# Folding the carried state into the decay's first column, in five scans of each pass

## The chip, the cores and the metric

The kernel runs on one core of a Trainium2 chip. The metric is the time of one execution on the device, in microseconds; the median of several runs is compared. The core has engines that work side by side and wait for each other by semaphores: TensorE (PE) multiplies matrices into PSUM, VectorE (DVE), ScalarE (ACT) and GpSimd (POOL) work on elements, SyncE (SP) issues the transfers. Each engine takes its instructions in order.

## The reference, cut to what matters

The network has two layers, each a state-space mixer and an MLP, on a picture of 64 x 64 tokens with 96 channels. The change concerns the mixer of layer 1. For each of 192 inner channels and 16 states it runs a recurrence over all 4096 tokens, in four directions: by rows, by columns, and both backward.

```python
def step(h, inp):
    u_t, dt_t, B_t, C_t = inp
    dA = jnp.exp(dt_t[..., None] * A)
    h = dA * h + (dt_t * u_t)[..., None] * B_t[:, None, :]
    y = jnp.sum(h * C_t[:, None, :], axis=-1)
    return (h, y)
_, ys = jax.lax.scan(step, h0, (uT, dT, BT, CT))
```

So a state is the decay times the state before, plus an input. The four directions' states are summed for each token, multiplied by C, summed over the 16 states, and gated.

## The kernel before, in words

**Tiles.** 192 channels times 16 states are 3072 recurrences. They are worked off in 24 passes of 128 (6 groups of 32 channels, 4 passes of 4 states in each). A pass holds 128 partitions by 4096 tokens, and cuts the tokens into four parts of 1024 (`SC`), so that each of the four directions is four scans, 16 in a pass. One scan is one VectorE instruction at line 1998: `tensor_tensor_scan` with multiply and add, on a decay tile in PSUM and an input tile in SBUF. Its fourth operand is where the running state starts: 0.0 for the first part of a direction, and for the others a column of a tile, the last state of the part before (128 partitions by 1 element).

**Chains and slots.** `o` tells rows (0) from columns (1), and `e` counts 0 to 7 along both ways: 0 to 3 forward (or backward, in turn), 4 to 7 the other way. `seq` alternates between the chains: column scan m, then row scan m - 2. Scan p of `seq` therefore continues scan p - 2. In this text a slot is the place of a scan in a pass, counted from the pass's first column scan: even slot s is the column scan e = s / 2, slots 1 and 3 are row scans 6 and 7 of the pass before, and slots 5, 7, 9, 11, 13 and 15 are row scans 0 to 5. Row or column scan 4 starts again from 0.0, as scan 0 does (slots 0, 5, 8 and 13). Scans e < 4 write into the tiles h0s and h1s, the later ones in place into their input (x0s, x1s, x2s for rows, in rotation; xws for columns).

**Decays.** `decay(p + 1)` is issued just behind `scan(p)` in the program (lines 2220 to 2222): ScalarE computes exp(dt times a rate) for the next scan into one of two PSUM tiles (`two`, da in the profile), which alternate. Its tile is the one that scan p - 1 reads, so it has to wait for that scan's end. Scan e = 4 reuses the decay tile of scan e = 3, over the same tokens the other way.

**What else is in the pass.** The other work is put behind numbered scans by a written plan (`put`, `spots`, `base`), in slots: four copies on ScalarE that permute the row input for the column scans (line 1968; slots 11, 13, 15, and 4 of the next pass); GpSimd's product of B and the input (1962), its sum of the two column directions (2003) and its product with C (2026); TensorE's sums of the directions through an identity matrix (2009 and 2013, from slot 14 into the next pass's slots 0 to 6); ScalarE's fetch of these sums from PSUM in eight halves (2022; slots 0, 1, 2, 3, 5, 6, 7, 9); TensorE's sum over states (2037). In two passes of each group of channels ScalarE and TensorE also compute the gate (2069; tanh at 2078 to 2080, in slot 12), and the end of a group adds a Copy with a scale (2090), a fetch (2096) and two products. In passes late in the kernel the first parts of the output product run beside (2121 to 2127). Loads are issued by SP in the order of the same plan.

**The end phase.** The last ten scans, from `first_late` on, and the output, the MLP and the stores are ordered by a planner (`Order`), which starts from costs and leads written into the program.

Of the kernel before, what the change touches and what calls it, by code (L numbers as in the profile page):

```python
# [33 lines left out]
AF = mybir.ActivationFunctionType  # L34
# [22 lines left out]
NS = 4  # L57
SC = L // NS
# [65 lines left out]
PAIRS = HW // 2  # L124

RELU0_ACT = [(c, 0) for c in range(8)]
IN_DVE, OTHERS = (), (15, 9, 9)


# [134 lines left out]
class Net:  # L264
# [832 lines left out]
    def keep(self, instruction):  # L1097
        self.tc.keep_in_program_order(instruction)
# [378 lines left out]
    def mlp0(self, c):  # L1477
# [18 lines left out]
        def rounded(m):  # L1496
            return lambda: keep(nc.scalar.copy(at["h16", c, m], at["h", c, m]))

        def relu(m):
            h, b = ("h16", c, m), b1[:, m : m + 1]  # L1500
            if (c, m) in RELU0_ACT:
                return lambda: keep(nc.scalar.activation(at[h], at[h], AF.Relu, bias=b))
            return lambda: keep(nc.vector.tensor_scalar(at[h], at[h], b, 0.0, ALU.add, ALU.max))

        def small(m):
            return lambda: keep(nc.gpsimd.tensor_copy(at["h8", c][:, m], at["h16", c, m], saturate=False))

        for m in range(nm):
            o.add("PE", 0.45, up(m), r=[xt], new={("h", c, m): "bank", **({} if m else {("h8", c): "h8"})})
            o.add("ACT", 0.58, rounded(m), r=[("h", c, m)], new={("h16", c, m): "h16"})  # L1510
            o.add(*(("DVE", 0.58), ("ACT", 0.73))[(c, m) in RELU0_ACT], relu(m), w=[("h16", c, m)])
            o.add("POOL", 0.72, small(m), r=[("h16", c, m), ("h8", c)], w=[("h8", c, m)])
# [371 lines left out]
    def scans(self, xs, out):  # L1884
# [13 lines left out]
        nc, tc, keep = self.nc, self.tc, self.keep  # L1898
        with ExitStack() as ctx:
# [7 lines left out]
            n, ns = len(passes), 4 * NS  # L1907
# [3 lines left out]
            hs, h0, h1, xw = self.hs, self.h0, self.h1, self.xw  # L1911
# [12 lines left out]
            seq = [(0, o, e) for o, e in first]  # L1924
# [3 lines left out]
            pos = {s: p for p, s in enumerate(seq)}  # L1928
            base = [pos[i + 1, 1, 0] - ns for i in range(last)] + [pos[last, 1, 0]]
            first_late = pos[last, 1, NS]  # L1930

            def slot(i, o, e):

                way = e // NS
                return way, (i + way) % 2 == 1, turn[i % 2][way][e % NS]

            das, accs, sums = {}, {}, {}
            two = [pa.tile([P, SC], F32, tag=f"da{j}", name=f"da{j}") for j in range(2)]
# [31 lines left out]
            def decay(p):  # L1970
                i, o, e = seq[p]
                if e == NS:

                    das[p] = das[pos[i, o, e - 1]]
                    return
                das[p] = 1 - das[p - 1] if p else 0
                decay_into(p)

            def decay_into(p):
                i, o, e = seq[p]  # L1980
                g, k = passes[i]
                t, j = two[das[p]], slot(i, o, e)[2]
                keep(nc.scalar.activation(t, dts[o][:, part[j]], AF.Exp, scale=self.a6[:, g, k : k + 1]))  # L1983

            def rows(i, j):
                return xs[2] if i == 0 and j < 2 else h0

            def scan(p):
                i, o, e = seq[p]
                way, back, j = slot(i, o, e)  # L1990
                x = (xs[i % 3], xw)[o]
                h = x if way else h1 if o else rows(i, j)
                to, da, x = h[:, part[j]], two[das[p]], x[:, part[j]]
                if back:
                    to, da, x = to[:, ::-1], da[:, ::-1], x[:, ::-1]
                at = (j + 1) * SC if back else j * SC - 1
                start = 0.0 if e % NS == 0 else (h if way or o else rows(i, j - 1 + 2 * back))[:, at : at + 1]
                keep(nc.vector.tensor_tensor_scan(to, da, x, start, ALU.mult, ALU.add))  # L1998

            def add_columns(i, a):  # L2000
# [167 lines left out]
            for i in range(n):  # L2168
# [22 lines left out]
                at = base[i - 1] if i else 0  # L2191
# [28 lines left out]
            for p in range(first_late):  # L2220
                scan(p)
                decay(p + 1)
                for f, args in plan.pop(p, []):
                    f(*args)
            assert not plan
            for p in range(first_late + 1, len(seq)):
                i, o, e = seq[p]
# [4 lines left out]
            at = od.at  # L2232
# [64 lines left out]
            for p in range(first_late, len(seq)):  # L2297
                i, c, e = seq[p]
                if p > first_late and e != NS:
                    od.add("ACT", 1.12, lambda p=p: decay_into(p), w=[("da", das[p])], table="exp")  # L2300
                od.add("DVE", 2.33, lambda p=p: scan(p), r=[("da", das[p]), ("S", c, e - 1)], w=[("S", c, e)])
# [4 lines left out]
            for p in (len(seq) - 2, len(seq) - 1):  # L2306
                i, c, e = seq[p]
# [22 lines left out]
            for a in range(NS):  # L2330
                j = turn[last % 2][1][a]
# [14 lines left out]
                else:  # L2346
                    t = hs[:, part[j]]
# [3 lines left out]
                    for h in range(nh):  # L2351
                        e, cost = ((dve, 1.2), (pool, 1.5))[a in TIMES_POOL]
# [224 lines left out]
```

## Time and profile before

| What | Value |
|---|---|
| median of 3 runs | 1230.8 us (1229.6 to 1230.89) |
| the profiled execution's own time | 1231.9 us |
| its span, first to last instruction | 1229.9 us |
| TensorE clock granted, mean | 0.877 of full speed |
| VectorE busy | 1134.9 us, 92% |
| TensorE busy | 1013.7 us, 82% |
| ScalarE busy | 881.8 us, 72% |
| GpSimd busy | 842.4 us, 68% |
| scans of layer 1 at line 1998 | 382, from 306.7 us to 1174.4 us |

The profile is one execution. A group of it is a line of the program with its engine, its operation, its operands by name (out, then in) and its shape, with the count and the durations. The timeline lists instructions by their start; what stands in brackets is how long the engine had been idle before and what ended that. The chain that ended last is followed back from the last instruction to what released each step. Scans in place (x0s<-da,x0s) don't show by name whether they begin with a constant or a column; those into h0s and h1s do, because the column is of the same tile.

### The profile page before, as it was taken

The page shows a single profiled execution, that of the slowest core. Times are in us where ns is not written, and L with a number is a line of the kernel's source. Part 1 is how long each engine was busy: PE and PEld are TensorE (multiplying, and loading weights), DVE is VectorE, ACT ScalarE, POOL GpSimd, SP SyncE. Part 2 cuts the span into 40 slices and gives each one's busy share as a digit, 9 for nine tenths or more (in the row PEclk, how much of TensorE's full clock was granted, in tenths as well). Part 3 has the DMA queues.
Part 4 walks back from the last instruction along what each step waited for, and adds up shares of the span by engine and source line. Part 5 has one row for each costly group of instructions (what it writes and reads, how often), then busy time and mean ns, then how long its engine had stood idle before and what let it go on. Part 6 is the DMA issues. An engine that isn't in the chain of part 4 may idle for free.

```text
span 1229.9 us, 11118 instructions
## 1 busy us (share of the span) xinstructions
PE 1013.7 (82%) x3498; PEld 414.7 (34%) x3498; DVE 1134.9 (92%) x908; ACT 881.8 (72%) x1065; POOL 842.4 (68%) x510
## 2 busy tenths in 40 slices
PE   9997889985278877887787877889778889888986
PEld 5533334321023322222332222233224444343344
DVE  7895787788898999999999999999999999999968
ACT  5682555656568878877888777878878878887626
POOL 3002364352678888888798878987798888886756
PEclk9998989995589887889978788988789999988987
DMA  2252010476763573575734585545736766432201
GB/s 76 67 174 53 1 27 20 124 245 193 235 193 126 182 237 125 172 230 172 239 112 127 194 258 166 180 146 185 233 115 194 246 195 235 142 101 83 103 1 52
DMA packets 79132, 183.14 MB, mean 149 GB/s; under 512 B 21534, under 2 KB 34936, under 8 KB 77688
## 3 DMA queue, kind: packets, MB, share of 16 engines
q1 hardware_dynamic: 78376, 182.16, 47.6%
q8 instruction: 29, 0.48, 0.2%
q14 instruction: 39, 0.32, 0.1%
q10 hardware_dynamic: 688, 0.19, 0.1%
HBM read 159.73 MB, written 21.52 MB: 147 GB/s over the span
## 4 chain that ended last, share of the span: by engine, by line
DVE 46%; issue 11%; PE 10%; ACT 5%; DMA 2%; POOL 1%; SPq 0%; another core or an unknown queue 0%; DVEq 0%; POOLq 0%; ACTq 0%
DVE h1s L1998 14%; DVE xws L1998 13%; DVE h0s L1998 8%; PE hs L2009 4%; DVE x2s L1998 3%; DVE x0s L1998 3%; DVE x1s L1998 3%; PE hs L2013 2%; ACT da L1983 2%; ACT xws L1968 2%; DMA x2s<-bc 1%; PE eo L2123 1%; PE da L2326 1%; POOL hss L2003 1%; DMA kept<-xn 1%
## 5 line engine op out<-in xcount | busy, mean ns | idle before, releaser
L2026 POOL TENSOR_TENSOR kept<-kept,kept 128x1024 f32<-128x1024 f32 x92 | 216.7, 2356 | 82.3 <-issue 40.2
L2003 POOL TENSOR_TENSOR hss<-h1s,xws 128x1024 f32<-128x1024 f32 x96 | 228.0, 2377 | 55.2 <-DVE xws L1998 52.4
L2009 PE MATMUL hs<-h0s,ident 128*128 128x512 f32 x360 | 222.9, 705 | 27.6 <-DVE h0s L1998 24.0
L1983 ACT ACTIVATE da<-dt1s,a 128x1024 f32<-128x1024 f32 x168 | 187.5, 1117 | 71.3 <-DVE xws L1998 55.3
L1998 DVE TENSOR_TENSOR_SCAN xws<-da,xws 128x1024 f32<-128x1024 f32 x96 | 221.6, 2308 | 10.4 <-ACT da L1983 10.3
L1983 ACT ACTIVATE da<-dt0s,a 128x1024 f32<-128x1024 f32 x166 | 185.1, 1115 | 45.1 <-DVE h0s L1998 16.2
L2013 PE MATMUL hs<-hss,ident 128*128 128x512 f32 x368 | 188.1, 603 | 15.4 <-POOL hss L2003 15.3
L1998 DVE TENSOR_TENSOR_SCAN h1s<-da,h1s,xws 128x1024 f32<-128x1024 f32 x72 | 167.3, 2323 | 0.3
L2037 PE MATMUL acc<-kept,fold 128*32 128x512 f32 x368 | 87.6, 687 | 73.8 <-POOL kept L2026 73.8
L2022 ACT COPY kept<-hs 128x512 f32<-128x512 f32 x184 | 107.1, 582 | 47.0 <-PE hs L2013 46.3
L2009 PEld LDWEIGHTS hs<-h0s,ident 128*128 128x128 f32 x360 | 71.5, 216 | 152.4 <-issue 82.3
L2013 PEld LDWEIGHTS hs<-hss,ident 128*128 128x128 f32 x368 | 70.0, 194 | 116.2 <-issue 79.1
L2009 PE MATMUL hs<-x1s,ident 128*128 128x512 f32 x128 | 75.5, 675 | 14.1 <-DVE x1s L1998 14.1
L2009 PE MATMUL hs<-x0s,ident 128*128 128x512 f32 x128 | 73.6, 659 | 14.8 <-DVE x0s L1998 14.8
L1962 POOL TENSOR_TENSOR x1s<-x1s,dus 128x1024 f32<-128x1024 f32 x32 | 75.5, 2361 | 9.0 <-DMA x1s<-bc 9.0
L2009 PE MATMUL hs<-x2s,ident 128*128 128x512 f32 x120 | 69.1, 660 | 14.1 <-DVE x2s L1998 14.1
L1962 POOL TENSOR_TENSOR x2s<-x2s,dus 128x1024 f32<-128x1024 f32 x32 | 75.7, 2364 | 2.7 <-DMA x2s<-bc 2.7
L1998 DVE TENSOR_TENSOR_SCAN x0s<-da,x0s 128x1024 f32<-128x1024 f32 x32 | 73.9, 2310 | 1.1 <-ACT da L1983 1.1
L1998 DVE TENSOR_TENSOR_SCAN x1s<-da,x1s 128x1024 f32<-128x1024 f32 x32 | 73.9, 2308 | 1.1 <-ACT da L1983 1.1
L1998 DVE TENSOR_TENSOR_SCAN x2s<-da,x2s 128x1024 f32<-128x1024 f32 x32 | 73.9, 2311 | 0.6 <-ACT da L1983 0.4
L1968 ACT COPY xws<-x1s 128x1024 f32<-128x1024 f32 x32 | 63.2, 1974 | 5.4 <-POOL hss L2003 5.4
L1968 ACT COPY xws<-x2s 128x1024 f32<-128x1024 f32 x32 | 63.2, 1976 | 4.2 <-POOL x2s L1962 4.2
(374 smaller groups left out, 1887.3 us busy)
## 6 DMA issues: line engine op xcount, KB each, us to landing
kept<-bc SPq DMA_DIRECT2D x92, 512.0 KB
x2s<-bc SPq DMA_DIRECT2D x32, 512.0 KB
x0s<-bc SPq DMA_DIRECT2D x28, 512.0 KB
x1s<-bc SPq DMA_DIRECT2D x28, 512.0 KB
dus<-du SPq DMA_DIRECT2D x20, 512.0 KB
dt1s<-dt SPq DMA_DIRECT2D x20, 512.0 KB
dt0s<-dt SPq DMA_DIRECT2D x20, 512.0 KB
kept<-xn SPq DMA_DIRECT2D x24, 384.0 KB
```

What stands on the lines that cost most here:

```text
L1962: keep(nc.gpsimd.tensor_tensor(x, x, du[:, part[j]], ALU.mult))
L1968: keep(copy(grid(xw)[:, w, :], cols(xs[i % 3])[:, w, :]))
L1983: keep(nc.scalar.activation(t, dts[o][:, part[j]], AF.Exp, scale=self.a6[:, g, k : k + 1]))
L1998: keep(nc.vector.tensor_tensor_scan(to, da, x, start, ALU.mult, ALU.add))
L2003: keep(nc.gpsimd.tensor_tensor(cols(hs)[:, w, :], grid(h1)[:, w, :], grid(xw)[:, w, :], ALU.add))
L2009: keep(nc.tensor.matmul(t, self.ident, x[:, chunk(m)], start=k == 0, stop=False))
L2013: keep(nc.tensor.matmul(sums[i, m], self.ident, hs[:, chunk(m)], start=False, stop=True))
L2022: keep(nc.scalar.copy(to, sums.pop((i, j * (SC // CH) + h))))
L2026: keep(nc.gpsimd.tensor_tensor(t, t, times_c_by(i, a), ALU.mult))
L2037: keep(nc.tensor.matmul(to, self.fold4, src, start=k == 0, stop=k == NK - 1))
L2123: keep(nc.tensor.matmul(o[:, j], y[:, j:CH:4], w, start=False, stop=j == 3))
L2326: keep(nc.tensor.matmul(o[:, j], y[r, 2 * k + j : CH : 4], w[r], start=first and j == 0, stop=end and j == 1))
```

## The change

In five slots of a pass (2, 3, 4, 7 and 9) the scan begins with the constant 1.0 and no longer with the carried column. So that the result is the same, ScalarE first multiplies the first column of the decay tile (the last one, for a backward scan) by the carried column: the scan's first step is then 1.0 times (decay times state), plus the input. The multiplication is a Copy with a scale for each partition, on 128 x 1 elements in place in PSUM, issued right behind the decay of that scan. `CARRIED` names the slots, counted from another origin ((p - 14) modulo 16, so 0, 1, 2, 5, 7). Scans 0 and 4, which start a direction, and scan 3, whose decay tile is read again by scan 4, are kept out by a condition, as are the first pass's early scans and the end phase; 112 scans are left.

```diff
+CARRIED = (0, 1, 2, 5, 7)
...
             first_late = pos[last, 1, NS]
+            carried = [p for p in range(ns, first_late) if (p - 14) % ns in CARRIED and seq[p][2] not in (0, NS - 1, NS)]
...
+            def carry(p):
+                i, o, e = seq[p]
+                way, back, j = slot(i, o, e)
+                at = (j + 1) * SC if back else j * SC - 1
+                h = (xs[i % 3], xw)[o] if way else h1 if o else rows(i, j - 1 + 2 * back)
+                return h[:, at : at + 1]
+
+            def carry_into(p):
+                if p in carried:
+                    at = SC - 1 if slot(*seq[p])[1] else 0
+                    t = two[das[p]][:, at : at + 1]
+                    keep(nc.scalar.activation(t, t, AF.Copy, scale=carry(p)))
...
-                at = (j + 1) * SC if back else j * SC - 1
-                start = 0.0 if e % NS == 0 else (h if way or o else rows(i, j - 1 + 2 * back))[:, at : at + 1]
+                start = 0.0 if e % NS == 0 else 1.0 if p in carried else carry(p)
                 keep(nc.vector.tensor_tensor_scan(to, da, x, start, ALU.mult, ALU.add))
...
             for p in range(first_late):
                 scan(p)
                 decay(p + 1)
+                carry_into(p + 1)
                 for f, args in plan.pop(p, []):
                     f(*args)
```

## The prediction

> **What bounds the kernel now.** I read the page first, its busy times and its chain that ended last:
>
> ```profile
> PE 1013.7 (82%) x3498; PEld 414.7 (34%) x3498; DVE 1134.9 (92%) x908; ACT 881.8 (72%) x1065; POOL 842.4 (68%) x510
> DVE 46%; issue 11%; PE 10%; ACT 5%; DMA 2%; POOL 1%; SPq 0%; another core or an unknown queue 0%; DVEq 0%; POOLq 0%; ACTq 0%
> ```
>
> VectorE is both the busiest engine and the main part of the chain. Next, the view of the scan's line (count; shortest/median/longest ns; first and last start), and the same for the two scans of another line:
>
> ```profile
> L1998 DVE TENSOR_TENSOR_SCAN h1s<-da,h1s,xws x72: 2319/2322/2349, 309.1 to 1144.8; 128x1024 f32<-128x1024 f32 x72
> L1998 DVE TENSOR_TENSOR_SCAN h1s<-da,xws x24: 2259/2260/2279, 306.7 to 1131.5; 128x1024 f32<-128x1024 f32 x24
> its engine sat idle before it (us, times) until:
>   ACT da L1983: 13.0, 11
> L1832 DVE TENSOR_TENSOR_SCAN x2s<-x1s,x0s x1: 2282/2282/2282, 297.3 to 297.3; 128x1024 f32<-128x1024 f32 x1
> L1832 DVE TENSOR_TENSOR_SCAN x2s<-x1s,x2s,x0s x1: 2350/2350/2350, 299.7 to 299.7; 128x1024 f32<-128x1024 f32 x1
> ```
>
> A scan that begins with a column of a tile takes 2322 ns, one that begins with the constant 0.0 takes 2260: 62 ns less, 68 at line 1832. All 382 scans idle for only 13 us in front of them. The timeline of VectorE in one pass says whether the 62 ns are also steps of the chain (start, duration):
>
> ```profile
> 412.83 2.26 DVE L1998 TENSOR_TENSOR_SCAN h1s<-da,xws 128x1024 f32<-128x1024 f32 x1
> 415.01 2.32 DVE L1998 TENSOR_TENSOR_SCAN x2s<-da,x2s 128x1024 f32<-128x1024 f32 x1
> 417.26 2.32 DVE L1998 TENSOR_TENSOR_SCAN h1s<-da,h1s,xws 128x1024 f32<-128x1024 f32 x1
> 419.50 2.32 DVE L1998 TENSOR_TENSOR_SCAN x2s<-da,x2s 128x1024 f32<-128x1024 f32 x1
> 421.74 2.32 DVE L1998 TENSOR_TENSOR_SCAN h1s<-da,h1s,xws 128x1024 f32<-128x1024 f32 x1
> ```
>
> They are: 2.18 us from start to start after the constant form, 2.24 after the other, each starting a little before the one ahead has ended. A pass of 12 and 4 takes 35.63 us (412.83 to 448.46), so x and x - 0.061 with 16x - 0.244 = 35.63: 2.242 and 2.181 us.
>
> What ScalarE does meanwhile, for slots 4 to 6 of that pass, and its dependent pair in another pass:
>
> ```profile
> 419.61 1.12 ACT L1983 ACTIVATE da<-dt1s,a 128x1024 f32<-128x1024 f32 x1 [0.61 <-DVE h1s L1998]
> 420.76 0.59 ACT L2022 COPY kept<-hs 128x512 f32<-128x512 f32 x1
> 421.85 1.12 ACT L1983 ACTIVATE da<-dt0s,a 128x1024 f32<-128x1024 f32 x1 [0.51 <-DVE x2s L1998]
> 422.91 1.98 ACT L1968 COPY xws<-x0s 128x1024 f32<-128x1024 f32 x1
> 424.79 1.12 ACT L1983 ACTIVATE da<-dt1s,a 128x1024 f32<-128x1024 f32 x1
> ...
> 505.98 0.39 ACT L2079 ACTIVATE kept<-z 128x256 f32<-128x256 f32 x1
> 506.41 0.51 ACT L2080 ACTIVATE kept<-kept,columns 128x256 f32<-128x256 f32 x1
> ```
>
> The decay of a slot starts when the scan two slots earlier has ended (417.26 + 2.32 = 419.58) and gives back its buffer. It is ready at 420.73, and its scan starts at 421.74: 1.01 us to spare. I worked this spare time out for every slot of passes 1 to 22. In the five slots of the change it is 0.92 to 1.01 us, but for four of slot 2 (0.46, 0.60, 0.68, 0.77) and one of slot 9 (0.89). The tight slots are others: slot 6, behind the permuting copy (0.20 to 0.25), slots 1 and 15 (about 0.27).
>
> **What the Trainium skill says.** (1) "DVE: scalar operands, raw-bit mode, write accounting and state across instructions", section Scalar operands: a scalar is either a [P,1] operand read per partition or a constant inside the instruction. It gives no price; the two forms in the trace do. (2) "VectorE: DVE Perf Modes", section The DRAIN you can't avoid: an instruction that reads what the one before it on its engine wrote needs a semaphore, which costs nothing extra on VectorE. For ScalarE the trace has 0.04 us between the dependent pair above (505.98 + 0.39 to 506.41). (3) "ScalarE: Activation LUTs", section Table sets: copy is in every table set, so a Copy between two Exp loads no table. The trace agrees: line 2090's Copy runs between decays without a load.
>
> **The change, part by part.**
> *Removed:* 112 scans lose the column operand. Slots 2, 3, 4, 7 and 9 (column scans 1 and 2, the row scan 7 of the pass before, row scans 1 and 2), in 22 or 23 passes each: 22 + 22 + 23 + 23 + 22. At 0.061 us: 6.83 us of VectorE. That 1.0 is as cheap as 0.0 isn't shown; both are constants of the instruction, so I take the whole 0.061 (ends: 0 and 0.068).
> *Added:* 112 ScalarE instructions on one column, with a per-partition scale, in place in PSUM. No row has this shape. By "ScalarE: Activation LUTs", section What ACT_TABLE_LOAD costs, 186 ns + 0.833 per element + 93 for a pointer operand is 280 ns as an estimate (the same formula gives 1132 for the decay, which takes 1118). The nearest row, line 2400 with 4 columns and a pointer, takes 299. With 0.02 to 0.04 behind the decay I take c = 0.32 us; ends 0.19 (the page's overlap of 93 ns taken off) and 0.42 (PSUM read as well as written). ScalarE's busy time grows by some 33 us.
> *On the path?* Its column comes from the scan two slots earlier, for whose end the decay has waited anyway, so it adds no wait but the one on its decay. Its own scan keeps 0.92 - 0.32 = 0.60 us to spare; the worst slot 2 keeps 0.14. Queued behind it are a fetch (line 2022) and the next decay. Behind slot 4's, from 419.61 on: the fetch can start 1.05 + c later, the next decay 0.48 after that, at 1.53 + c. That decay's buffer now comes free 2.18 after 419.61, so up to c = 0.65 nothing moves. Past that it would delay slot 6, whose spare 0.20 falls to 0.14 because scan 4 is shorter: slot 6 stalls from c = 0.79. The fetch feeds POOL's product and PE's second buffer; PE is at the next half chunk then. Where PE paces that fetch, in the worst pass (698.1), the decay is late by 0.04 us and slot 6 keeps 0.12. So at both ends of c the cost is nothing; the cover is ScalarE's idle 0.5 to 0.6 us in front of each decay. Without that cover it would be 112 x 0.32 = 36 us.
> *Waits:* the scan waits for ScalarE as before, for a later instruction. Later writers of the carried column must also wait for ScalarE's read, long past. Line 1998 has 194 semaphore instructions of 21 ns in VectorE's queue, without a mark on the 2.24 steps. I take 0.
> *Where the gain is given back:* wherever a chain that does not pass through VectorE ends in one of the stalls. One of them, in the view of the chain:
>
> ```profile
> 479.73 5.31 PE hs L2009 x6
> ...
> 504.96 6.40 DMA kept<-xn
> ```
>
> and where it ends, in VectorE's timeline:
>
> ```profile
> 517.70 2.35 DVE L1998 TENSOR_TENSOR_SCAN x2s<-da,x2s 128x1024 f32<-128x1024 f32 x1 [0.15 <-ACT da L1983]
> ```
>
> From 479.73 PE sums without pause until 504.95, then the gate's input is loaded and ScalarE's tanh steps follow, and slot 15 waits. Earlier scans in that pass only wait longer here: all 5 places are lost. Likewise pass 1 (stall at 372.0, PE from 337.6): 3. The stalls at 945.6, 981.3, 1088.4 and 1126.3 begin with scan slot 8 (929.66, 965.68, 1072.66, 1111.37): slot 9 is lost in each, 4. The stall at 1152.3 in the end phase follows PE sums from 1133.7: the last 4. Together 16 of 112, 0.98 us.
> *Sum:* 96 x 0.061 = 5.86 us. The profiled execution has a span of 1229.9 and a time of 1231.9, 1.1 above the median of the runs: 1231.9 - 5.9 = 1226.0 for it, and 1230.8 - 5.9 = 1224.9 on the median. I say 1225.0 us (-0.47%). What a measurement here can tell from no change is about 0.2%, 2.5 us.
>
> **Rivals.**
> *A, absorbed:* PE is 82% busy, and in gate passes VectorE already waits for it. If the shorter passes (35.32) run into PE's sums, POOL's products or late fetches in all 12 passes with tanh steps instead of 6, 12 x 5 = 60 of the 112 places are lost: 52 x 0.061 = 3.2, or 1227.6; if other passes are hit too, 1229. Against it: in the 6 others slot 14 keeps its full 0.93 to 0.95.
> *B, no saving:* the constant 1.0 may cost what the column costs, or the shorter form only owe its time to being a chain's first. Then 1230.8. Against it: line 1832 and both directions show the same difference.
> *C, slower:* the in-place multiply waits for PSUM's acknowledgment much longer than the pair above for SBUF's. Its place is between decay and scan, in all five slots. It decides from c = 1.02, where the spare of about 0.98 and the gained 0.061 are used up (0.02 of hand-over counted). At c = 1.1 each place loses 0.08, 112 x 0.08 = 9 us: 1240. For it: no row shows a PSUM read behind a PSUM write on ScalarE. Against it: that would be more than three times any small ScalarE row.
> *D, more:* PE's clock (0.877 on average) falls elsewhere against the passes and some of the 10 us of stalls vanish: 1222.
>
> **How the numbers follow.** Forecast (4.5 to 7 us saved) 0.64; A 0.14, of it 0.08 clear of 2.5 us; B 0.06; C 0.11; D 0.05. Faster 0.64 + 0.08 + 0.05 = 0.77, same 0.06 + 0.06 = 0.12, slower 0.11. The range leaves out C, B and half of D, some 0.2: from 1222.8 to 1229.3 us. The forecast alone: 1223.7 to 1226.3.
>
> **What would show it.** Right: 45 of the 72 scans h1s<-da,h1s,xws lose their column operand and take 2260; a pass takes 35.32 us; a new ScalarE group of 112 at about 0.3 us, with nobody waiting long for it; the stall at slot 15 of the pass that began at 484 grows from 0.24 to about 0.5. Wrong: constant-one scans at 2320 (B), VectorE idle before slots 2, 3, 4, 7, 9 or 6 in most passes (C), or new stalls in slots 14 and 15 of many gate passes (A).

## The result and the profile after

The changed kernel takes 1225.6 us, the median of 12 runs (1223.4 to 1232.9), against 1230.85 for the kernel before (12 runs, 1227.6 to 1235.3). The ratio is 0.9964, with an interval of 0.9948 to 0.9979: 0.36% faster, 4.4 us, give or take 1.9. A repetition gave 1225.2 us and 0.9959 (0.9944 to 0.9974). The profiled execution took 1229.0 us, one of the longer ones; its span is 1227.0, 2.9 below that of before.

The page's busy times, and its chain that ended last:

```profile
PE 1016.3 (83%) x3498; PEld 415.0 (34%) x3498; DVE 1128.4 (92%) x908; ACT 905.9 (74%) x1177; POOL 841.3 (69%) x510
DVE 38%; PE 16%; issue 9%; ACT 7%; DMA 3%; POOL 1%; another core or an unknown queue 0%; DVEq 0%; SPq 0%; POOLq 0%; ACTq 0%
```

VectorE has lost 6.5 us of work, ScalarE has gained 24.1 us and 112 instructions. The chain leans less on VectorE (46% before) and more on TensorE (10% before). That says nothing yet of the gain: in the version further down that only adds the multiplications, and is no faster, VectorE has 37% of the chain and TensorE 14%. The scan is at line 2012 now, the decay at 1985, the fetch at 2036, the permuting copy at 1970. The view of the scan's line, cut (shortest/median/longest ns):

```profile
L2012 DVE TENSOR_TENSOR_SCAN h1s<-da,xws x69: 2262/2268/2273, 307.0 to 1137.3; 128x1024 f32<-128x1024 f32 x69
...
L2012 DVE TENSOR_TENSOR_SCAN h1s<-da,h1s,xws x27: 2324/2330/2350, 309.3 to 1141.7; 128x1024 f32<-128x1024 f32 x27
...
its engine sat idle before it (us, times) until:
  ACT da L1985: 15.8, 13
```

45 of the 72 column scans with a carried column have become constant ones, and the two forms differ by the same 62 ns. Every scan is 6 to 8 ns longer in this trace than in that of before, the untouched ones too; the steps from start to start are not. The view of the new line, 2001, cut to one of its five groups:

```profile
L2001 ACT ACTIVATE da<-da,h1s x45: 236/236/238, 346.0 to 1136.4; 128x1 f32<-128x1 f32 x45
...
who waited for it (us, times):
  PEld hs L2023: 0.5, 2
```

236 ns each, and no scan is recorded as waiting for it. Now the steps, in VectorE's timeline of pass 3 (the passes count from 0; it is the pass whose timeline the prediction shows), from slot 2 on, with a stall that wasn't there before:

```profile
417.12 2.26 DVE L2012 TENSOR_TENSOR_SCAN h1s<-da,xws 128x1024 f32<-128x1024 f32 x1
419.30 2.27 DVE L2012 TENSOR_TENSOR_SCAN x2s<-da,x2s 128x1024 f32<-128x1024 f32 x1
421.49 2.26 DVE L2012 TENSOR_TENSOR_SCAN h1s<-da,xws 128x1024 f32<-128x1024 f32 x1
423.67 2.27 DVE L2012 TENSOR_TENSOR_SCAN h0s<-da,x0s 128x1024 f32<-128x1024 f32 x1
426.59 2.35 DVE L2012 TENSOR_TENSOR_SCAN h1s<-da,h1s,xws 128x1024 f32<-128x1024 f32 x1 [0.66 <-ACT da L1985]
```

Slots 2, 3 and 4 now take 2.18 us from start to start. Then slot 6 comes 0.74 us late. ScalarE in the same pass:

```profile
415.17 1.12 ACT L1985 ACTIVATE da<-dt1s,a 128x1024 f32<-128x1024 f32 x1
416.33 0.24 ACT L2001 ACTIVATE da<-da,h1s 128x1 f32<-128x1 f32 x1
416.49 0.59 ACT L2036 COPY kept<-hs 128x512 f32<-128x512 f32 x1
...
421.93 0.59 ACT L2036 COPY kept<-hs 128x512 f32<-128x512 f32 x1 [0.70 <-PE hs L2027]
422.41 1.12 ACT L1985 ACTIVATE da<-dt0s,a 128x1024 f32<-128x1024 f32 x1
...
425.37 1.12 ACT L1985 ACTIVATE da<-dt1s,a 128x1024 f32<-128x1024 f32 x1
```

The decay of slot 2 ends at 416.29, the multiplication follows 0.04 later and is done at 416.57: c = 0.28 us. The fetch behind it starts 1.32 us after the decay's start, where 1.05 was usual. The stall of slot 6 has another reason: the fetch at 421.93 had waited 0.70 us for TensorE, and the decay behind it, the permuting copy and the decay of slot 6 (425.37) were late with it.

To compare traces I use two sums. The stretch is from the first scan's start to the last one's. The stalls are what each step exceeds 2.242 us by (2.181 after a constant), where that is over 0.06; the first four steps of the kernel are left out.

| | stretch, us | ordinary pass, us | stalls, us |
|---|---|---|---|
| before | 867.7 | 35.63 | 18.3 |
| after | 864.5 | 35.32 | 21.9 |

Between these two traces, the 112 places saved 112 x 0.061 = 6.83 us of steps; the stalls grew by 3.6; 3.2 are left. They grew by 0.74 in pass 3 (slot 6), 0.59 in pass 5, 0.64 in pass 17, 0.28 in pass 18, 0.88 in pass 22, and by less elsewhere. The stall at the end of pass 5, which stood in the prediction with 0.15 us of idle time, is now

```profile
518.02 2.35 DVE L2012 TENSOR_TENSOR_SCAN x2s<-da,x2s 128x1024 f32<-128x1024 f32 x1 [0.55 <-ACT da L1985]
```

### The profile page after: what moved, and what is told of

Read it like the earlier page. It is cut to its first block, busy times and chain, and to the rows that moved or that the text cites. A ratio compares the mean times of both kernels' runs of the same rounds, so it can differ in the third digit from the quotient of the medians.

```text
span 1227.0 us, 11219 instructions
## 1 busy us (share of the span) xinstructions
PE 1016.3 (83%) x3498; PEld 415.0 (34%) x3498; DVE 1128.4 (92%) x908; ACT 905.9 (74%) x1177; POOL 841.3 (69%) x510
## 4 chain that ended last, share of the span: by engine, by line
DVE 38%; PE 16%; issue 9%; ACT 7%; DMA 3%; POOL 1%; another core or an unknown queue 0%; DVEq 0%; SPq 0%; POOLq 0%; ACTq 0%
DVE xws L2012 11%; DVE h1s L2012 10%; PE hs L2023 7%; DVE h0s L2012 7%; PE hs L2027 4%; ACT da L1985 3%; DVE x2s L2012 3%; DVE x1s L2012 2%; DVE x0s L2012 2%; ACT xws L1970 2%; DMA kept<-xn 2%; DMA dt<-hss 1%; POOL hss L2017 1%; ACT kept L2036 1%; PE acc L2051 1%
## 5 line engine op out<-in xcount | busy, mean ns | idle before, releaser
L2012 DVE TENSOR_TENSOR_SCAN h1s<-da,xws 128x1024 f32<-128x1024 f32 x69 | 156.5, 2268 | 0.0
L1964 POOL TENSOR_TENSOR x0s<-x0s,dus 128x1024 f32<-128x1024 f32 x28 | 66.3, 2368 | 0.0
```

What stands on the lines that cost most here:

```text
L1964: keep(nc.gpsimd.tensor_tensor(x, x, du[:, part[j]], ALU.mult))
```

## The experiments

Diffs are against the changed kernel, unless said otherwise.

**The constant alone.**

```diff
-                carry_into(p + 1)
```

> The 112 scans begin with the constant 1.0, but the multiplication on ScalarE is left out, so the carried state is missing from these scans. My theory (the gain is VectorE's 0.061 us per place, ScalarE's part is nearly free, the rest is given back in stalls that TensorE paces): an ordinary pass of 35.32 us as with the change, and a time within 1.5 us of the changed kernel's, 1224 to 1226. Rival 1 (ScalarE's added work costs a good part of the gain): 3 us or more faster than the changed kernel, 1222 or less. Rival 2 (a constant saves nothing): 1231, as before.

Measured: 1225.6 us, ratio to before 0.9956 (0.9936 to 0.9975); ordinary passes 35.32 us. This is the changed kernel's time without any of its work on ScalarE. The interval, 1222.9 to 1227.7 us, leaves out rival 1's 1222 and rival B's 1230.8.

**The multiplication alone.**

```diff
-                    keep(nc.scalar.activation(t, t, AF.Copy, scale=carry(p)))
+                    keep(nc.scalar.activation(t, t, AF.Copy, scale=self.one))
...
-                start = 0.0 if e % NS == 0 else 1.0 if p in carried else carry(p)
+                start = 0.0 if e % NS == 0 else carry(p)
```

> The scans keep their column operand; ScalarE does the 112 extra instructions in the same places, but multiplies by a column of ones. My theory: 1231, within 1.5 us of before, passes of 35.63 us. Rival 1: 1233 or more. An extra instruction takes 236 ns in both.

Measured: 1231.45 us, ratio 0.9998 (0.9983 to 1.0014); passes of 35.63 us. 112 instructions of 236 ns cost nothing that can be measured; the interval reaches from 2.1 us less to 1.7 us more. Its trace has stalls of 20.2 us, with VectorE's steps unchanged: 2 us more than the trace of before, at the same time within the interval.

**Every place.**

```diff
-                carry_into(p + 1)
...
-                start = 0.0 if e % NS == 0 else 1.0 if p in carried else carry(p)
+                start = 0.0 if e % NS == 0 else 1.0 if ns <= p < first_late else carry(p)
```

> Every scan from the second pass to the end phase begins with a constant (1.0 in place of each column) and nothing is multiplied, so the carried state is missing in all of them. 268 places at 0.061 us are 16.3 us of VectorE's time, and an ordinary pass is 16 x 2.181 = 34.90 us. My theory: some 48 places lie between the start of a chain without VectorE and a stall and are lost, so 13 us are left, 1218; if the six other passes with tanh steps stall too, 9 us, 1222. Rival 2: 1231. Rival 3 (TensorE or another engine is the bound as soon as passes are shorter than 35.3): 1225, no better than the change, with idle time before many scans.

Measured: 1218.6 us, ratio 0.9907 (0.9886 to 0.9929). VectorE's timeline, first scans of two passes:

```profile
410.98 2.26 DVE L2012 TENSOR_TENSOR_SCAN h1s<-da,xws 128x1024 f32<-128x1024 f32 x1
...
445.88 2.26 DVE L2012 TENSOR_TENSOR_SCAN h1s<-da,xws 128x1024 f32<-128x1024 f32 x1
```

34.90 us, 16 x 2.181. 12.2 of 16.3 us arrive, between the 13 and the 9 expected; a part of them may come from the granted clock, 0.883 on average in these six runs and 0.877 in those of the kernel before. TensorE and the others are not the bound of an ordinary pass even there, and the 0.061 us hold for all 12 places of a pass. The stalls are 23.0 us in this trace.

**Twice the work on ScalarE, and four times.**

```diff
                     keep(nc.scalar.activation(t, t, AF.Copy, scale=carry(p)))
+                    keep(nc.scalar.activation(t, t, AF.Copy, scale=self.one))
```

and with the added line three times, in a loop.

> The change with every multiplication on ScalarE followed by a second one by a column of ones, so c (from the decay's end to the end of the last of them) is 2 x 0.28 = 0.56 us. The prediction's limits were 0.65 for the decay of slot 5, 0.79 for a stall of slot 6, 0.92 to 1.01 for the five slots themselves. My theory: still free, 1224.5 to 1227, ordinary passes of 35.32 us. Rival 1 (ScalarE's work counts): 1229 or more.

> Four dependent instructions in each place (the multiplication and three by ones), c = 1.12 us. My theory: past the spare of 0.94 to 1.01; each place waits some 0.15 to 0.2 us for ScalarE, and slot 6 another 0.3: 112 x 0.17 + 22 x 0.3 = 26 us slower than the change, 1250 (1240 to 1260), with line 2001 as releaser in front of scans in all five slots. If the spare is larger than I read from the trace: below 1235.

Measured: twice 1225.5 us, ratio 0.9946 (0.993 to 0.9961), most passes at 35.32 or up to 0.12 above; c is 0.54 us. Four times 1265.2 us, ratio 1.0261 (1.023 to 1.0291). So the cover is there: a second multiplication costs nothing that the times show. Some cost can't be ruled out: four passes with the gate (2, 6, 10 and 14) got stalls of 0.1 us in slot 15 that the traces of the change don't have, and the 12 runs had a granted clock of 0.886 on average, against 0.878 for the kernel before, which may hide a cost of 1 or 2 us. (An estimate: by the two groups of runs at the end of this section, 0.008 of clock goes with some 3 us.) Four times is far past the limit. But it is 15 us worse than I expected. Its ScalarE and its VectorE in pass 3:

```profile
418.50 1.13 ACT L1985 ACTIVATE da<-dt0s,a 128x1024 f32<-128x1024 f32 x1
...
419.93 0.77 ACT L2003 ACTIVATE da<-da,columns 128x1 f32<-128x1 f32 x3
...
421.10 1.13 ACT L1985 ACTIVATE da<-dt1s,a 128x1024 f32<-128x1024 f32 x1
```

```profile
420.74 2.29 DVE L2014 TENSOR_TENSOR_SCAN x2s<-da,x2s 128x1024 f32<-128x1024 f32 x1 [0.24 <-ACT da L2003]
423.41 2.29 DVE L2014 TENSOR_TENSOR_SCAN h1s<-da,xws 128x1024 f32<-128x1024 f32 x1 [0.38 <-ACT da L2003]
```

From decay to decay ScalarE now takes 2.60 us (418.50 to 421.10), more than a scan's 2.18, in three neighbouring slots that each also hold a fetch. ScalarE became the bound there, and the lateness adds up (0.17, 0.35, 0.49 us of stall in slots 2, 3 and 4 of that pass). I had counted each place by itself. Slot 6, for which I had counted 0.3 us, stalled by 0.1; from pass 9 on slot 2 stalled by 0.5 to 0.8 us in eleven passes, which I didn't follow. A pass took 36.9 us and more.

**TensorE relieved.** Early parts of the output product left out, of the kernel before and of the changed one:

```diff
-                steps = [(load_y, load)] + ([(early_out, (i, 9 + k)), (early_fetch, (i, 10 + k))] if i < last else [])
+                steps = [(load_y, load)]
```

> The kernel before without the early parts of the output product in passes 17 to 22 (their matmuls on TensorE and the copies back; this part of the output is missing). My theory that the stalls of these passes are paced by TensorE's early products: the stalls in slots 14 and 15 of passes 17, 18, 21 and 22, some 6 us, shrink to under 1 us: 1225. If something else paces them (gate loads, POOL): 1230.

> The changed kernel without the same early products. My theory: with TensorE relieved, fewer of the 112 places are lost (3 in pass 1, 5 in pass 5, 4 in the end), so it is 6.1 us faster than the kernel before without them, 1219, where the change with them gave some 5. If the places are lost elsewhere: 4 us or less.

Measured: without them, the kernel before takes 1225.8 us (0.9945 of before, 0.9925 to 0.9966) and the changed kernel 1222.3 (0.9916, 0.9893 to 0.9939). In the trace of the first, the stalls of passes 18, 21 and 22 are gone, 5.4 us in the trace of before; pass 17 has 1.4 instead of 0.4. So those stalls come from the early products, as expected, except in pass 17. The edit takes away ScalarE's copies of these products as well as TensorE's matmuls. Which of the two paces the stall is in ScalarE's timeline of the changed kernel, for slot 14 of pass 22:

```profile
1121.10 0.37 ACT L2092 COPY kept<-z 128x256 f32<-128x256 f32 x1 [2.29 <-PE z L2083]
...
1122.20 1.10 ACT L1985 ACTIVATE da<-dt1s,a 128x1024 f32<-128x1024 f32 x1
```

ScalarE, with the late decay still to do, sits idle for 2.29 us until TensorE, behind its early products, has made the gate's product z: it is TensorE. The second half, whether the change gains more without them, is not settled: the two differ by 3.5 us in the medians (6 runs each), and the two intervals together leave some 4 us either way, so neither 6.1 nor 4 is excluded. The two traces differ by 7.2 us in the stretch (865.7 and 858.5).

**Seven places in every pass, and in the passes without tanh steps only.**

```diff
-CARRIED = (0, 1, 2, 5, 7)
+CARRIED = (0, 1, 2, 5, 7, 8, 10)
```

and, with the first line as it was (one line, cut at both ends),

```diff
-... (p - 14) % ns in CARRIED and ...
+... (p - 14) % ns in (CARRIED + ((8, 10) if ((p + 4) // ns) % NK in (0, 3) else ())) and ...
```

> The change with slots 10 and 12 added, column scans 5 and 6, which had 1.01 us to spare before the change. 45 places more, an ordinary pass of 35.20 us. My theory: 12 of the 45 lie ahead of known stalls, 33 x 0.061 = 2.0 us faster than the changed kernel, 1223.5. Rival 1: ScalarE's extra work in slots 9 to 13, where passes with tanh steps are tight, takes it back: 1226 or more, with longer stalls in slots 14 and 15.

> The change with slots 10 and 12 added only in the passes that have no tanh steps (two of four), 22 places more than the change. My theory: 35.20 us in these passes and 35.32 in the others, nothing given back in slots 14 and 15, where the seven places everywhere brought nothing: 22 x 0.061 = 1.3 us faster than the change, 1224, which the runs can hardly tell from it. Rival 1 (ScalarE's added work counts): 1226 or more.

Measured: seven everywhere (44 places more; I had written 45) 1225.6 us, 0.9963 (0.9945 to 0.9981), in a trace with passes of 35.20 us. Two stalls are new, in slot 12, one of the added places, where the scan waits for the multiplication itself (0.3 us in pass 21, 0.2 in pass 22). Pass 9 has these two:

```profile
655.49 2.35 DVE L2012 TENSOR_TENSOR_SCAN xws<-da,xws 128x1024 f32<-128x1024 f32 x1 [0.58 <-ACT da L1985]
658.40 2.35 DVE L2012 TENSOR_TENSOR_SCAN x0s<-da,x0s 128x1024 f32<-128x1024 f32 x1 [0.56 <-ACT da L1985]
```

The 2.0 us expected did not show in the time. But that the added places made the stalls of pass 9 isn't shown: it stalls in traces without them too (0.33 us in the second trace of the change, 0.59 in the kernel before without early products), and the stalls of this trace, 21.2 us in all, are no more than the 21.9 of the first trace of the change. In the passes without tanh steps only (20 places more; I had written 22): 1223.9 us, 0.9951 (0.9933 to 0.9969), passes of 35.20 and 35.32, two and two in turn. It has the lowest median of the versions that compute all of the reference, but the interval doesn't part it from the change, whose repetition in the same series had 1225.2.

**The change once more.**

> The changed kernel once more, for a second trace of it. My theory (the stall of 0.74 us in slot 6 of pass 3 came from TensorE's clock at that moment): ordinary passes of 35.32 us again, but that stall is gone or in another pass, and the sum of all stalls from the first pass on differs from the first trace's 21.9 us by 1 us or more. Rival (ScalarE's work makes that stall, a property of the program): 0.7 us in slot 6 of pass 3 again. The time: 1224 to 1227.

Measured: 1225.2 us, 0.9959 (0.9944 to 0.9974). This trace, of an execution of 1220.8 us, has a stretch of 860.4 and stalls of 17.8 us, 4.0 less than the first trace of the same program. Everything in pass 3 comes some 2.2 us, a slot, earlier here. TensorE's sums at its start, in the first trace and in this one, with this one's slot 6:

```profile
413.06 3.30 PE L2027 MATMUL hs<-hss,ident 128*128 128x512 f32 x4 [1.86 <-POOL hss L2017]
```

```profile
411.29 1.88 PE L2027 MATMUL hs<-hss,ident 128*128 128x512 f32 x4
423.67 2.33 DVE L2012 TENSOR_TENSOR_SCAN h1s<-da,h1s,xws 128x1024 f32<-128x1024 f32 x1
```

The same four matmuls took 3.30 us and 1.88 us, and slot 6, which starts at 423.67 here, follows slot 5 (421.49) at 2.18 without a stall. So that stall belongs to the moment, not to the program: ScalarE's orders and instructions are the same. The traces have a reason, the granted clock while these four ran: 0.58 in the first and 1.00 in this one (1.00 in the trace of before too, for 1.99 us). That GpSimd's sum, which the first of them waited for, was late is not it: counted from the pass's first scan they began at 0.36 us in the first trace and at 0.76 in this one.

Pass 22 shows the same. Its stall waits for TensorE's early products and gate products, which run there without a pause. They took 8.62 us in the trace of before (from 1115.36 on, granted clock 0.75) and 9.43 in the first of the change (from 1111.59 on, 0.59), which is 0.81 of the 0.88 us by which the stall grew. In the second trace they took 8.62 again (0.72), and the stall is longer than before by 0.06 us, one place, as the prediction has it. The 12 runs of the change point the same way (five with a mean granted clock of 0.880 or more average 1224.7 us, four with 0.874 or less 1228.8), but no run here set the clock, and a low mean can be an effect as well: without the early products, where TensorE has less to do, it was 0.868 in runs that were faster.

## Why the prediction was right, point by point

Predicted 1225.0 us, measured 1225.6 (1226.4 by the ratio); the range and the sign held. The profiled execution, for which the working gave 1226.0, took 1229.0.

*The saving of 0.061 us at 112 places.* Right: passes of 35.32 us as worked out, and 34.90 with every place. That 1.0 is as cheap as 0.0, which no row of before showed, is shown: the constant alone gives the whole gain. Rival B fell.

*ScalarE's multiplication at c = 0.32 us.* 0.28 us measured, the instruction itself 236 ns where the formula of the Trainium skill's page "ScalarE: Activation LUTs", section What ACT_TABLE_LOAD costs, gave 280 as an estimate. The growth of ScalarE's busy time, 33 us in the prediction, was 24.1. The 33 are 112 times 0.295, near the 299 ns of the row with four columns; at 236 ns they would have been 26.4.

*Free at both ends of c.* Right: the multiplication alone moved nothing (0.9998), and twice the work nothing that the times show. The spare of the five slots and the 0.14 us left to slot 6 (median 0.17 in the trace after, 0.14 at least where it doesn't stall) were read well. The limit itself, c = 1.02, for rival C was too simple: with neighbouring slots the limit is also that the decay, the multiplications and the fetch together fit in 2.18 us. By the trace, decay and fetch need 1.05 + 0.48 = 1.53 of it, which leaves 0.65 (with c = 1.07 in four times the work, 1.53 + 1.07 are the 2.60 us found). This is the same 0.65 that I had set for slot 4 alone; I should have carried it through slots 2, 3 and 4. No run has a c between 0.54 and 1.07, so where the loss begins is not measured.

*What is given back, 16 places, 0.98 us.* This step holds in the sum and only partly in its parts, and that the sum fits to 0.6 us is in part luck. Going by the medians, 1230.85 - 1225.6 = 5.3 of 6.83 arrive, so 1.6 is given back; by the ratio, 2.4 with an interval of 0.4 to 4.2. But of the two traces of the changed kernel, one has 3.6 us more of stalls than the trace of before and the other 0.5 less. I took the stalls of one trace as the kernel's own. They differ by 4 us between executions of one program and by 2 us between two programs with the same steps on VectorE, more than the whole term. Pass 5 was to stall about 0.5 us and had 0.82 in one trace, 0.44 in the other; pass 3's stall in slot 6 was not foreseen, though its mechanism was (a fetch that TensorE paces, and slot 6's small spare). One part can be read clear of this, the last four places. The stall at 1152.3 in the end phase, before and after:

```profile
1152.26 2.35 DVE L1998 TENSOR_TENSOR_SCAN xws<-da,xws 128x1024 f32<-128x1024 f32 x1 [0.71 <-ACT da L1983]
```

```profile
1149.30 2.35 DVE L2012 TENSOR_TENSOR_SCAN xws<-da,xws 128x1024 f32<-128x1024 f32 x1 [0.94 <-ACT da L1985]
```

It grew by 0.23 us, 4 x 0.061 within rounding. It has 0.95 in the second trace of the change, in that of the constant alone and in that of twice the work, and 0.71 in that of the multiplication alone: what VectorE gains there is waited away, as worked out. How many of the 112 places are lost on average is still open. What the traces do show is which waits take them: TensorE's sums, early products and gate products, by way of ScalarE's queue.

*The rivals.* A (the six other gate passes absorb the gain too, 1227.6) did not come: of the six, only pass 9 stalled, by 0.33 us, and in one of the two traces. C (slower) fell with c at 0.28. D (1222, TensorE's clock falls otherwise) came in single executions, as in the second trace at 1220.8, and not in the median.

## What to carry to other kernels

Where a chain of equal instructions sets the time, compare their forms by the step from start to start: an operand that costs 0.06 us is worth moving when another engine is idle at that moment and would wait for the same release anyway. Read that engine's spare per slot, and check it over neighbouring slots together, since lateness adds up. And do not price the stalls of a kernel from one trace: run it twice, and see which of them are the same.

## What was not expected of the hardware

A scaled copy of 128 x 1 in place in PSUM, behind the exponential that wrote it, took 236 ns, began 0.04 us after it, and let the next independent ScalarE instruction start only 0.16 us after its own start: a dependent one-column instruction cost 0.27 us of ScalarE's order (1.32 instead of 1.05 us). Four TensorE matmuls of one shape took 1.88 us in one execution, at a granted clock of 1.00, and 3.30 in another of the same program, at 0.58.
